# Seven block products for the last batch's outputs as well, and earlier or later places for three groups of sums

## The chip, the cores and the metric

The kernel runs on one core of a Trainium2 chip. The core has five engines that run their own instruction streams and meet at semaphores: TensorE (PE in the profile, its weight loads PEld) multiplies matrices, VectorE (DVE), ScalarE (ACT) and GpSimd (POOL) work on tiles, and SyncE (SP) issues the transfers. Each stream is in order: an instruction that waits holds everything behind it on its engine. On-chip data lie in SBUF, results of TensorE in PSUM. The metric is device time in microseconds of one execution, lower is better; all arithmetic is in float32.

## The reference

There are 8 batches of 256 tokens of width 1024, and 32 heads of width 32. Keys and values are the same tensor, 256 rows for each batch.

```python
mu, var = mean(hidden), var(hidden)
x = (hidden - mu) * rsqrt(var + 1e-05) * ln_gamma + ln_beta
Q = split_heads(x @ Wq.T)                      # 8, 32, 256, 32
K = V = split_heads(memory)
scores = einsum('bhsd,bhtd->bhst', Q, K) * 32 ** -0.5
scores = where(mask, scores, -inf)
attn = einsum('bhst,bhtd->bhsd', softmax(scores), V)
out = hidden + merge_heads(attn) @ Wout.T
```

## The kernel before

**Slots.** The work is cut into 64 slots, eight for each batch; a slot is four heads of one batch. Slot n (the loop at L887) issues the scores of slot n + 1 (L479), the value products of slot n - 2 (L622), a piece of the previous batch's output product and a piece of the query product of a later batch, all on TensorE, and the softmax of slot n + 1 on the other engines. Batch b's own slots are 8b to 8b + 7; its outputs are computed in the eight or nine slots after them.

**Softmax.** For each head VectorE adds the mask bias and takes the maximum of the (negated) scores (L515), ScalarE takes the exponential with its sum (L519), VectorE the reciprocal of the sum (L526), GpSimd multiplies (L528), and VectorE transposes 32x32 blocks (L534). ScalarE copies a part aside (L540) and SyncE moves blocks between partitions by four transfers (L600, L604; the loads of the slot, called `between`, go out in the middle). ScalarE also copies attended values from PSUM (`copy_at`, L635).

**Products by seven.** Where two matrices are cut in 2x2 blocks, their product is made from seven block products instead of eight, with sums of blocks ahead and behind. For the queries of batches 3 to 7 the blocks of x are summed on GpSimd (`sum_x`, L430): S1 = A21 + A22, S2 = S1 - A11, S4 = A12 - S2, S3 = A22 - S2. The seven products (L440) of a batch lie in seven successive slots, the first of them two slots into the batch before it. For the outputs of batches 0 to 6 the same is done with the attended values (`sum_at`, L675; products at L694 in `product_steps`), where S3 = A11 - A21, S2 = A22 - S3, S1 = S2 + A11, S4 = A12 - S2. Token halves are the rows, halves of the 1024 inner columns the columns of A; Wout is cut in B11, B12, B21, B22, from which T1 to T4 are built by GpSimd in the first slots (`sum_wo`), T1 in the place of B12. The same sums of the query weights (`sum_wq`, L391) are written over the weights; three blocks are stored in DRAM and come back through the tile `ring` (`keep_wq`, `load_ring`).

**Order of outputs.** In a batch's second slot TensorE makes A11 x B11 for the batch before (po_A, L694), ScalarE copies it to p1 (`keep_p1`, L702), and only then TensorE may go on adding A12 x B21 into the same PSUM tile. Other sums are added from PSUM by VectorE (L732, L736) or from p1 by GpSimd (L727) to the residual tiles `r`.

**Normalized x.** SyncE loads x, VectorE takes its statistics (L226) and block transpose (L311), and 16 transfers (`move_x`, L327) bring the blocks to their partitions (tile xnT). The tables `moves`, `sums`, `away` and `rings` say by hand in which slot each step is issued. For batches 4 to 7, S1 of x is issued at the end of the slot before a batch's first, for the next batch; S2 at the end of the first slot, after S3 of the attended values; S4 and the S2 of the values in the second. For batch 3 its S1 is in slot 16, and S2 and S4 in slot 17.

**The last batch.** Its outputs are plain: for two token halves and two column halves, eight products of 128x512 each (`project`, L744). B12 is loaded again into the query weights' place (`load_b12`, L753). Four products of the first output are made inside the loop; the others follow it, with the values of slots 62 and 63 between them. The residual is loaded into `again` (L1013) after the loop; VectorE adds (L736, L1037) and SyncE stores. The last output is split into 384 and 128 columns.

Of the kernel before, what the change touches and what calls it, by code (L numbers as in the profile page):

```python
# [46 lines left out]
F32 = mybir.dt.float32  # L47
U8 = mybir.dt.uint8
AF = mybir.ActivationFunctionType
ALU = mybir.AluOpType  # L50

P = 128
# [7 lines left out]
def xattn_kernel(  # L60
# [11 lines left out]
    nc = tc.nc  # L72
    B, S, D = x.shape
    T = mask.shape[2]
    HD = D // HEADS
    NC = D // P
    NQ = NC
    NH = P // HD
    NS = S // P
    NT = T // P  # L80
    NO = D // 512
# [5 lines left out]
    N = B * NQ  # L87

    const = ctx.enter_context(tc.tile_pool(name="const", bufs=1))
    xp = ctx.enter_context(tc.tile_pool(name="xp", bufs=2))  # L90
# [12 lines left out]
    ps_s = ctx.enter_context(tc.tile_pool(name="ps_s", bufs=4, space=PS))  # L103
    ps_v = ctx.enter_context(tc.tile_pool(name="ps_v", bufs=2, space=PS))
    ps_q = ctx.enter_context(tc.tile_pool(name="ps_q", bufs=1, space=PS))
    ps_o = ctx.enter_context(tc.tile_pool(name="ps_o", bufs=1, space=PS))

    NK = D // P // 2
    ring = const.tile([P, NK, NK, P], F32, tag="ring", name="ring")
# [13 lines left out]
    xs, ks, vs, rs = {}, {}, {}, {}  # L123
# [300 lines left out]
    def sum_x(b, name):  # L424

        one, two, op = {
            "S1": ("A21", "A22", ALU.add), "S2": ("S1", "A11", ALU.subtract),
            "S4": ("A12", "S2", ALU.subtract), "S3": ("A22", "S2", ALU.subtract),
        }[name]
        nc.gpsimd.tensor_tensor(x_part(b, name), x_part(b, one), x_part(b, two), op)  # L430
# [229 lines left out]
    def operand(b, name):  # L660

        if name in ("S2", "S1"):
            return s2s[b]
        s, k = {"A11": (0, 0), "A12": (0, 1), "A21": (1, 0), "A22": (1, 1),
                "S3": (1, 0), "S4": (0, 1)}[name]
        return ats[b, k][:, :, s].rearrange("p c a k -> p c (a k)")

    def sum_at(b, name, c=slice(0, NK)):
        if name == "S2" and c.start == 0:
            s2s[b] = up.tile([P, NK, P], F32, tag="s2", name=f"s2_{b}")  # L670
        one, two, op = {
            "S3": ("A11", "A21", ALU.subtract), "S2": ("A22", "S3", ALU.subtract),
            "S1": ("S2", "A11", ALU.add), "S4": ("A12", "S2", ALU.subtract),
        }[name]
        nc.gpsimd.tensor_tensor(  # L675
            operand(b, name)[:, c], operand(b, one)[:, c], operand(b, two)[:, c], op
        )
# [56 lines left out]
    def store(b, s, h, po=None):  # L734
        r = rs.pop((b, s, h))
        nc.vector.tensor_tensor(r, pos[b] if po is None else po, r, ALU.add)  # L736
        nc.sync.dma_start(out[b, ts(s, P), ts(h, 512)], r)

    def project(po, b, s, h, chunks, cols=slice(0, 512)):

        for c in chunks:
            k, i = divmod(c, NK)
            w = {(0, 0): wo[:, B11], (1, 0): wo[:, B21], (1, 1): wo[:, B22], (0, 1): b12}[k, h]
            nc.tensor.matmul(  # L744
                po, ats[b, k][:, i, s].rearrange("p a k -> p (a k)"), w[:, i, cols],
                start=(c == 0), stop=(c == NC - 1),
            )


    b12 = wq[:, :2].rearrange("p o c q -> p (o c q)").rearrange("p (c q) -> p c q", c=NK)  # L750

    def load_b12(c):
        nc.sync.dma_start(b12[:, c], woT[ts(c, P), ts(1, 512)])  # L753

# [19 lines left out]
    for b in range(1, B):  # L776
        first = NQ * (b - 1) + 2
        if b == 1:
            when = dict(moves=())
        elif b == 2:  # L780
            when = dict(
                loads=(0, 1), stats=(2, 3), norms=(3, 3), trans=(4, 5),
                moves=tuple(5 + i // 4 for i in range(16)),
            )
        else:
            when = dict(
                loads=(first - 12, first - 11) if b == SPLIT else (first - 13, first - 12),
                stats=(first - 10, first - 9) if b == SPLIT else (first - 11, first - 9),
                norms=(first - 8, first - 7), trans=(first - 7, first - 6),
                moves=tuple(first - 6 + (i + 2) // 6 for i in range(16)),  # L790
            )
        for table, key in (
            (loads, "loads"), (stats, "stats"), (norms, "norms"), (trans, "trans"),
        ):
            for i, n in enumerate(when.get(key, ())):
                assert n < first
                table[n].append((b, i))
        for n in range(N):
            part = [i for i, slot in enumerate(when["moves"]) if slot == n]
            if part:  # L800
                assert n < first - 1
                moves[n].append((b, part))
        biases[NQ * b - 2].append(b)
        if b % 2 == 0:
            masks[NQ * b - 7].append(b)
# [7 lines left out]
    ):  # L813
        sums[n] += [partial(sum_wo, which, c) for c in chunks]
    for n, which, *chunks in (
        (9, "T1", 0), (14, "T1", 1, 2), (15, "T1", 3), (15, "T3", 0, 1), (16, "T3", 2),
        (18, "T3", 3), (19, "T2", 0), (20, "T2", 1, 2, 3), (21, "T4", 0, 1), (22, "T4", 2, 3),
    ):
        sums[n] += [partial(sum_wq, which, o) for o in chunks]


    away, rings = {n: [] for n in range(N)}, {n: [] for n in range(N)}
    for n, name, half in (
        (9, "B11", 0), (10, "B11", 1), (15, "T1", 0), (16, "T1", 1), (16, "T3", 0), (19, "T3", 1),
    ):
        away[n].append(partial(keep_wq, name, half))
    for n, b in firsts.items():
# [53 lines left out]
    def project_steps(n, place):  # L881
        for one in steps.get((n, place), ()):
            product_steps(*one)


    last = None
    for n in range(N):  # L887
        b, i = divmod(n - NQ, NQ)
        new_q = new_qs[n]
# [15 lines left out]
        if n < NQ:  # L905
# [1 line left out]
                (B12, 0), (B22, 0), (B11, 0), (B12, 1), (B22, 1), (B11, 1), (B21, 0), (B21, 1)  # L907
            )[n]
            between.append(partial(load_wo, which, pair))
        if N - NQ <= n < N - NQ + NK:  # L910
            between.append(partial(load_b12, n - (N - NQ)))

        if n + 1 < N:
            scores(n + 1)
# [51 lines left out]
        for one in biases[n]:  # L966
            mask_bias(one)
        project_steps(n, 2)
        if b >= 0:
            for name in {0: ("S3",), 2: ("S4",), 3 if b == B - 2 else 5: ("S1",)}.get(i, ()):  # L970
                sum_at(b, name)
            if i == 0 and b == B - 2:
                sum_at(b, "S2", slice(0, NK - 1))
        for slot, name in ((n + 3, "S1"), (n + 2, "S2"), (n + 1, "S4"), (n - 1, "S3")):
            if slot in firsts and firsts[slot] > SPLIT:
                sum_x(firsts[slot], name)
        for slot, name in ((n + 2, "S1"), (n + 1, "S2"), (n + 1, "S4"), (n - 1, "S3")):
            if firsts.get(slot) == SPLIT:
                sum_x(SPLIT, name)
        if b == B - 2:  # L980
            if i > 2:
                add_kept(b, i, *ENDS_TO[i])
# [9 lines left out]
            fold(n)  # L992
        for one in sums[n]:
            one()
        if not new_qs[n] and N - NQ + 2 < n < N - 1:

            chunks = [c for c in range(NQ) if N - NQ + c <= n - 3]
            if last is None:
                last = ps_q.tile([P, 512], F32, tag="pq", name="po_last")
                made = 0  # L1000
            project(last, B - 1, 0, 0, chunks[made:])
            made = len(chunks)


    send(B - 2, *ENDS_TO[7])
    add_kept(B - 2, 2, *ENDS_TO[2])
    send(B - 2, *ENDS_TO[2])
    ends = [(B - 1, s, h) for h in range(NO) for s in range(NS)]
    pos = {end: ps_s.tile([P, 512], F32, tag="sc", name=f"po_{end[1]}_{end[2]}") for end in ends[1:]}
    pos[ends[0]] = last  # L1010
    again = xp.tile([P, NS, D], F32, tag="x", name="x_again")
    for s in range(NS):
        nc.sync.dma_start(again[:, s, :], x[B - 1, ts(s, P), :])  # L1013
    for b, s, h in ends:
        rs[b, s, h] = again[:, s, ts(h, 512)]
    project(pos[ends[1]], *ends[1], range(NK))
    project(last, *ends[0], range(made, NQ - 3))
    values(N - 2)
    copy_at(N - 2)
    project(pos[ends[1]], *ends[1], range(NK, NQ - 3))  # L1020
    project(pos[ends[2]], *ends[2], range(NK))
    project(last, *ends[0], (NQ - 3,))
    project(pos[ends[1]], *ends[1], (NQ - 3,))
    values(N - 1)
    copy_at(N - 1)
    project(pos[ends[2]], *ends[2], range(NK, NQ - 1))
    for i, end in enumerate(ends[:3]):
        project(pos[end], *end, range((NQ - 2, NQ - 2, NQ - 1)[i], NQ))
        store(*end, pos[end])

    b, s, h = ends[3]
    r = rs.pop(ends[3])
    for cols in (slice(0, 384), slice(384, 512)):
        po = pos[ends[3]] if cols.start == 0 else ps_v.tile([P, P], F32, tag="pv", name="po_end")
        po = po[:, : cols.stop - cols.start]
        project(po, *ends[3], range(NQ), cols)
        nc.vector.tensor_tensor(r[:, cols], po, r[:, cols], ALU.add)  # L1037
        nc.sync.dma_start(out[b, ts(s, P), ds(512 * h + cols.start, cols.stop - cols.start)], r[:, cols])


# [38 lines left out]
```

## Time and profile before

| what | value |
|---|---|
| median of 3 runs | 592.53 us (591.06 to 595.61) |
| the profiled execution | 590.59 us |
| its span, first to last instruction | 588.8 us |
| mean granted TensorE clock | 0.994 |
| TensorE busy | 572.1 us, 97% of the span |
| VectorE, ScalarE, GpSimd busy | 453.9, 412.1 and 396.7 us |
| transfers | 119.02 MB, mean 202 GB/s |

A row of a timeline gives start, length, engine, line, operation, output tile <- input tiles, shapes and the number of merged records; brackets hold the idle time of the engine before it and what ended that. One float32 product of 128x512 has two records, about 0.43 us each. In the list of waits, the numbers behind a pair are total us, times and the longest. A row by stretch gives the stretch, its length, then busy us and (records) for PE, PEld, DVE, ACT and POOL, the granted clock (1.00 is full speed), the share of the transfer engines and GB/s.

### The profile page before, as it was taken

What the parts mean: (1) busy time and instruction counts of PE and PEld (TensorE: products, weight loads), DVE (VectorE), ACT (ScalarE), POOL (GpSimd) and SP (SyncE); (2) the same over time, 40 slices, a digit from 0 to 9 for tenths busy, and PEclk for the clock granted to TensorE, in tenths of its full rate; (3) what the DMA queues carried; (4) which work ended last, traced back from release to release, by engine and by line L of the source; (5) the groups of instructions that cost most, each with busy time, mean ns of one, the idle gap of its engine ahead of it and who ended that gap; (6) DMA issues with size and microseconds to landing.
All of it is one profiled execution on the core that took longest, in us unless ns stands there. A gap on an engine that the chain in (4) does not pass through costs nothing.

```text
span 588.8 us, 20015 instructions
## 1 busy us (share of the span) xinstructions
PE 572.1 (97%) x7176; PEld 395.1 (67%) x7176; DVE 453.9 (77%) x1686; ACT 412.1 (70%) x1424; POOL 396.7 (67%) x663
## 2 busy tenths in 40 slices
PE   8999998999999999899999999799998999999997
PEld 8778884676676776577766776467774777754544
DVE  6898898787778887888888888678876778779801
ACT  4688877776578775796777877578775766769810
POOL 1787999789788985766576762857628466458720
PEclk9999999999999999999999999999998999999999
DMA  8675798755886777876878666776657764547661
GB/s 291 240 217 174 218 259 230 248 154 171 248 247 175 236 207 220 226 221 175 241 210 245 190 186 187 241 211 201 169 140 224 221 203 141 143 121 224 177 184 71
DMA packets 48051, 119.02 MB, mean 202 GB/s; under 512 B 9168, under 2 KB 9936, under 8 KB 47952
## 3 DMA queue, kind: packets, MB, share of 16 engines
q1 hardware_dynamic: 47664, 117.74, 67.8%
q8 instruction: 57, 0.93, 0.8%
q14 instruction: 42, 0.34, 0.2%
q10 hardware_dynamic: 288, 0.01, 0.0%
HBM read 66.33 MB, written 11.53 MB: 132 GB/s over the span
## 4 chain that ended last, share of the span: by engine, by line
PE 71%; DVE 7%; DMA 6%; POOL 6%; issue 4%; ACT 3%; SPq 2%; POOLq 0%; DVEq 0%; ACTq 0%
PE po_S L694 16%; PE pq L340 9%; PE pq_A L440 9%; PE sc L479 9%; PE pv L622 8%; PE po_A L694 7%; PE pq_S L440 6%; POOL e L528 4%; DMA pT<-pT 3%; PE po L744 3%; DVE pT L534 3%; ACT e L519 2%; DVE e L515 2%; DMA x<-in_x_dram 1%; PE po_last L744 1%
## 5 line engine op out<-in xcount | busy, mean ns | idle before, releaser
L528 POOL TENSOR_SCALAR e<-e,rden 128x256 f32<-128x256 f32 x512 | 236.4, 482 | 124.5 <-DVE rden L526 123.1
L519 ACT ACTIVATE e<-e,mn 128x256 f32<-128x256 f32 x512 | 254.0, 501 | 54.6 <-DVE mn L515 54.6
L534 DVE STREAM_TRANSPOSE pT<-e 128x512 f32<-128x512 f32 x256 | 180.8, 706 | 60.1 <-POOL e L528 51.1
L515 DVE CUSTOM_DVE_ANT_0 e<-sc,mb 128x256 f32<-128x256 f32 x512 | 186.0, 416 | 32.6 <-PE sc L479 32.3
L540 ACT COPY pc<-pT 128x512 f32<-128x512 f32 x128 | 79.0, 617 | 78.9 <-DVE pT L534 39.8
L519 ACT ACTIVATION_READ_ACCUMULATOR e<-e,mn 128x1 f32 x512 | 97.8, 191 | 0.0
L340 PE MATMUL pq<-xnT,wq 128*128 128x256 f32 (+1 forms) x368 | 84.2, 383 | 2.4 <-DMA xnT<-xe 2.4
L340 PEld LDWEIGHTS pq<-xnT,wq 128*128 128x128 f32 x368 | 68.6, 190 | 17.1 <-issue 3.8
L479 PEld LDWEIGHTS sc<-k,qa 32*128 32x128 f32 x1024 | 46.4, 185 | 43.6 <-issue 25.5
L622 PE MATMUL pv<-pT,v 64*32 64x128 f32 x4096 | 74.5, 274 | 0.0
L694 PE MATMUL po_S<-wo,at 128*128 128x512 f32 x152 | 74.3, 606 | 0.0
L622 PEld LDWEIGHTS pv<-pT,v 64*32 64x32 f32 x4096 | 57.2, 105 | 25.3 <-issue 11.9
L479 PE MATMUL sc<-k,qa 32*128 32x256 f32 x1024 | 74.0, 402 | 0.1
L694 PE MATMUL po_A<-wo,at 128*128 128x512 f32 x128 | 63.9, 635 | 9.6 <-ACT p L702 8.1
L694 PE MATMUL po_S<-wo,s 128*128 128x512 f32 x104 | 50.1, 605 | 0.0
L694 PEld LDWEIGHTS po_A<-wo,at 128*128 128x128 f32 x128 | 23.2, 195 | 36.0 <-issue 22.8
L515 DVE DVE_READ_ACCUMULATOR2_ANT mn<- 128x1 f32 x512 | 42.6, 83 | 0.0
L526 DVE RECIPROCAL rden<-den 128x2 f32<-128x2 f32 x256 | 37.7, 147 | 5.7 <-ACT e L519 4.5
L440 PEld LDWEIGHTS pq_A<-xnT,wq 128*128 128x128 f32 x320 | 37.3, 192 | 4.8 <-issue 4.1
L694 PEld LDWEIGHTS po_S<-wo,at 128*128 128x128 f32 x152 | 25.8, 190 | 19.8 <-issue 19.1
L440 PE MATMUL pq_A<-xnT,wq 128*128 128x128 f32 x320 | 37.3, 275 | 0.0
L635 ACT COPY at<-pv 128x128 f32<-128x128 f32 x128 | 26.2, 254 | 10.3 <-PE pv L622 10.3
(89 smaller groups left out, 595.3 us busy)
## 6 DMA issues: line engine op xcount, KB each, us to landing
v<-in_kv_dram SPq DMA_DIRECT2D x32, 512.0 KB, 5.2
pT<-pT SPq DMA_DIRECT2D x128, 128.0 KB, 3.3
pT<-pc SPq DMA_DIRECT2D x128, 128.0 KB, 4.4
ring<-kept_T SPq DMA_DIRECT2D x18, 512.0 KB
k<-in_kv_dram SPq DMA_DIRECT2D x32, 256.0 KB, 3.9
x<-in_x_dram SPq DMA_DIRECT2D x14, 512.0 KB
r<-in_x_dram SPq DMA_DIRECT2D x28, 256.0 KB, 5.1
out_dram<-r SPq DMA_DIRECT2D x28, 256.0 KB, 3.0
```

The source lines that it names most:

```text
L340: nc.tensor.matmul(pqs[n], wq[:, o, c, :], xnTs[b](c), start=(c == 0), stop=(c == NC - 1),)
L440: nc.tensor.matmul(pqs[b][:, o, :], w[:, c], x_[:, c], start=begins and o + c == 0, stop=c == NK - 1, skip_group_check=True,)
L479: nc.tensor.matmul(scs[n][j][:, s, :], qa[r, n % NQ, ts(s, P)], ks[n - n % 2][r, n % 2, :], start=True, stop=True,)
L515: nc.vector.tensor_tensor_reduce(out=e[:, s, :], in0=pss[j][:, s, :], in1=mbs[n // NQ], scale=1.0, scalar=NO_SCORE, op0=ALU.add, op1=ALU.m ...
L519: nc.scalar.activation(e[:, s, :], e[:, s, :], AF.Exp, bias=mn[:, s : s + 1], scale=-1.0, accum_out=den[:, s : s + 1],)
L526: nc.vector.reciprocal(rden, dens[j])
L528: nc.gpsimd.tensor_scalar(es[j][:, s, :], es[j][:, s, :], rden[:, s : s + 1], 1.0, ALU.mult, ALU.mult,)
L534: nc.vector.transpose(pT[:, :, :, j, :, :].rearrange("p a i s k -> p (a i) s k"), es[j].rearrange("p s (b t) -> p b s t", t=K),)
L540: nc.scalar.copy(pc[:, :, ts(j, 2)], pT[:, 1, :, ts(j, 2)])
L622: nc.tensor.matmul(pvs[n][r][j * HD : (j + 1) * HD], vs[n - n % 2][ts(r, 2 * K), i, ds(n % 2 * P + j * HD, HD)], pT[ts(r, 2 * K), :, i, j, ...
L635: nc.scalar.copy(ats[b, k][:, c, :, ts(r, 2), :], pv.rearrange("p a s k -> p s a k"))
L694: nc.tensor.matmul(po, operand(b, name)[:, c], wo[:, which, c], start=begins and c == 0, stop=c == NK - 1, skip_group_check=not begins,)
```

## The change

Batch 7's outputs are made by the seven products too. Its S3 is issued in slot 62. A11 x B11 is still made in the loop, in the four places that the first output had. After the loop, ScalarE copies it to `end_p1` in `ring`, which is free by then; S2, S1 and S4 go to three more parts of `ring`, chunk by chunk as the attended values arrive: chunks 0 and 1 at once and chunk 2 on GpSimd, chunk 3 on VectorE. Products go in the order of the chunks' arrival; S2 x T2 of the last chunk is multiplied twice, into two sums. The residual is loaded in slot 60, and B12 is not loaded again.

Other places: S1 of x for batches 4 to 7 goes one slot later, to the batch's first slot, ahead of S2; batch 3's S2 goes to slot 16, one earlier. S3 of the attended values goes from the next batch's first slot to the batch's own seventh (batches 2 to 6), for batch 1 to its eighth; batch 0 keeps its place. The 16 moves of batch 2 go 4, 6 and 6 to slots 5, 6 and 7 instead of 4 each to slots 5 to 8. T3 of the query weights is summed one chunk in each of slots 15 to 18, and its first half stored in slot 17 instead of 16.

```diff
+    end_sums = {"S1": ring[:, 0], "S2": ring[:, 1], "S4": ring[:, 2]}
+    end_p1 = ring[:, 3].rearrange("p c q -> p (c q)")
...
+    def end_sum(chunks, engine):
+        for name, one, two, op in (
+            ("S2", "A22", "S3", ALU.subtract), ("S1", "S2", "A11", ALU.add),
+            ("S4", "A12", "S2", ALU.subtract),
+        ):
+            engine.tensor_tensor(
+                end_operand(name)[:, chunks], end_operand(one)[:, chunks],
+                end_operand(two)[:, chunks], op,
+            )
+
+    def end_steps(po, name, which, chunks, begins=(), cols=slice(0, 512)):
 
         for c in chunks:
...
             nc.tensor.matmul(
-                po, ats[b, k][:, i, s].rearrange("p a k -> p (a k)"), w[:, i, cols],
-                start=(c == 0), stop=(c == NC - 1),
-            )
...
+                po, end_operand(name)[:, c], wo[:, which, c, cols],
+                start=c in begins, stop=True, skip_group_check=True,
+            )
+
+    def end_add(r, po):
+        nc.vector.tensor_tensor(r, po, r, ALU.add)
...
-                moves=tuple(5 + i // 4 for i in range(16)),
+                moves=tuple(5 + (i + 2) // 6 for i in range(16)),
...
-        (9, "T1", 0), (14, "T1", 1, 2), (15, "T1", 3), (15, "T3", 0, 1), (16, "T3", 2),
-        (18, "T3", 3), (19, "T2", 0), (20, "T2", 1, 2, 3), (21, "T4", 0, 1), (22, "T4", 2, 3),
+        (9, "T1", 0), (14, "T1", 1, 2), (15, "T1", 3), (15, "T3", 0), (16, "T3", 1),
+        (17, "T3", 2), (18, "T3", 3), (19, "T2", 0), (20, "T2", 1, 2, 3), (21, "T4", 0, 1), (22, "T4", 2, 3),
...
+    S3_SLOTS = [(b, NQ * b + {0: NQ, 1: NQ - 1}.get(b, NQ - 2)) for b in range(B)]
...
-        (9, "B11", 0), (10, "B11", 1), (15, "T1", 0), (16, "T1", 1), (16, "T3", 0), (19, "T3", 1),
+        (9, "B11", 0), (10, "B11", 1), (15, "T1", 0), (16, "T1", 1), (17, "T3", 0), (19, "T3", 1),
...
-        if N - NQ <= n < N - NQ + NK:
-            between.append(partial(load_b12, n - (N - NQ)))
+        if n == N - 4:
+            again = xp.tile([P, NS, D], F32, tag="x", name="x_again")
+            for s in range(NS):
+                between.append(partial(nc.sync.dma_start, again[:, s, :], x[B - 1, ts(s, P), :]))
...
+        for one, slot in S3_SLOTS:
+            if n == slot:
+                sum_at(one, "S3")
         if b >= 0:
-            for name in {0: ("S3",), 2: ("S4",), 3 if b == B - 2 else 5: ("S1",)}.get(i, ()):
+            for name in {2: ("S4",), 3 if b == B - 2 else 5: ("S1",)}.get(i, ()):
                 sum_at(b, name)
...
-        for slot, name in ((n + 3, "S1"), (n + 2, "S2"), (n + 1, "S4"), (n - 1, "S3")):
-            if slot in firsts and firsts[slot] > SPLIT:
+        for slot, name in ((n + 2, "S1"), (n + 2, "S2"), (n + 1, "S4"), (n - 1, "S3")):
+            if slot in firsts:
                 sum_x(firsts[slot], name)
-        for slot, name in ((n + 2, "S1"), (n + 1, "S2"), (n + 1, "S4"), (n - 1, "S3")):
-            if firsts.get(slot) == SPLIT:
-                sum_x(SPLIT, name)
...
+    nc.scalar.copy(end_p1, last)
+    end_sum(slice(0, 2), nc.gpsimd)
+    nc.gpsimd.tensor_tensor(r00, r00, end_p1, ALU.add)
+    nc.gpsimd.tensor_tensor(r01, r01, end_p1, ALU.add)
...
+    for c in range(2):
+        end_steps(to_c11, "A12", B21, (c,), (0,))
+        end_steps(to_c21, "A22", T4, (c,), (0,))
     values(N - 2)
     copy_at(N - 2)
...
+    end_sum(slice(2, 3), nc.gpsimd)
+    end_steps(last, "S3", T3, range(NK))
+    end_add(r10, last)
+    end_add(r11, last)
+    s2t2 = ps_o.tile([P, 512], F32, tag="po", name="po_end_s2")
+    end_steps(s2t2, "S2", T2, range(2), (0,))
     values(N - 1)
     copy_at(N - 1)
...
+    end_sum(slice(3, 4), nc.vector)
+    first_cols, last_cols = slice(0, 384), slice(384, 512)
+    end_steps(to_c22, "S1", T1, range(2), (0,))
+    end_steps(s2t2, "S2", T2, (2,))
+    for r in (r01, r10, r11):
+        end_add(r, s2t2)
+    end_steps(to_c22, "S1", T1, (2,))
+    end_steps(to_c11, "A12", B21, (2,))
+    end_steps(to_c21, "A22", T4, (2,))
+    end_steps(to_c22, "S2", T2, (3,))
+    end_steps(to_c22, "S1", T1, (3,))
+    end_add(r11, to_c22)
+    end_store(1, 1)
+    end_add(r01, to_c22)
+    end_steps(to_c21, "A22", T4, (3,))
+    end_steps(to_c21, "S2", T2, (3,))
+    end_add(r10, to_c21)
+    end_store(1, 0)
+    end_steps(to_c11, "A12", B21, (3,))
+    end_add(r00, to_c11)
+    end_store(0, 0)
+
+    for cols in (first_cols, last_cols):
+        po = to_c12[:, cols] if cols.start == 0 else ps_v.tile([P, P], F32, tag="pv", name="po_end")
+        end_steps(po, "S4", B22, range(NK), (0,), cols)
+        end_add(r01[:, cols], po)
+        end_store(0, 1, cols)
```

More of the change, by code (lines that the diff above doesn't have):

```diff
@@ L737, in store, with end_operand @@
         nc.sync.dma_start(out[b, ts(s, P), ts(h, 512)], r)
-    def project(po, b, s, h, chunks, cols=slice(0, 512)):
+    end_sums = {"S1": ring[:, 0], "S2": ring[:, 1], "S4": ring[:, 2]}
+    end_p1 = ring[:, 3].rearrange("p c q -> p (c q)")
+    def end_operand(name):
+        return end_sums[name] if name in end_sums else operand(B - 1, name)
+    def end_sum(chunks, engine):
[8 more added lines that the diff above has]
+    def end_steps(po, name, which, chunks, begins=(), cols=slice(0, 512)):
         for c in chunks:
-            k, i = divmod(c, NK)
-            w = {(0, 0): wo[:, B11], (1, 0): wo[:, B21], (1, 1): wo[:, B22], (0, 1): b12}[k, h]
             nc.tensor.matmul(
-                po, ats[b, k][:, i, s].rearrange("p a k -> p (a k)"), w[:, i, cols],
-                start=(c == 0), stop=(c == NC - 1),
-            )
-    b12 = wq[:, :2].rearrange("p o c q -> p (o c q)").rearrange("p (c q) -> p c q", c=NK)
-    def load_b12(c):
-        nc.sync.dma_start(b12[:, c], woT[ts(c, P), ts(1, 512)])
+                po, end_operand(name)[:, c], wo[:, which, c, cols],
+                start=c in begins, stop=True, skip_group_check=True,
+            )
+    def end_add(r, po):
+        nc.vector.tensor_tensor(r, po, r, ALU.add)
     START = 3
@@ L883, in project_steps @@
             product_steps(*one)
-    last = None
     for n in range(N):
@@ L994, in xattn_kernel @@
             one()
-        if not new_qs[n] and N - NQ + 2 < n < N - 1:
-            chunks = [c for c in range(NQ) if N - NQ + c <= n - 3]
-            if last is None:
+        if N - NQ + 2 < n < N - 1:
+            c = n - (N - NQ + 3)
+            if c == 0:
                 last = ps_q.tile([P, 512], F32, tag="pq", name="po_last")
-                made = 0
-            project(last, B - 1, 0, 0, chunks[made:])
-            made = len(chunks)
+            end_steps(last, "A11", B11, (c,), (0,))
     send(B - 2, *ENDS_TO[7])
@@ L1007, in xattn_kernel @@
     send(B - 2, *ENDS_TO[2])
[L1008 to L1017, printed above, removed]
+    r00, r01, r10, r11 = (again[:, s, ts(h, 512)] for s in range(NS) for h in range(2))
@@ new lines, in end_store @@
+    def end_store(s, h, cols=slice(0, 512)):
+        nc.sync.dma_start(
+            out[B - 1, ts(s, P), ds(512 * h + cols.start, cols.stop - cols.start)],
+            again[:, s, ds(512 * h + cols.start, cols.stop - cols.start)],
+        )
[3 more added lines that the diff above has]
+    nc.gpsimd.tensor_tensor(r01, r01, end_p1, ALU.add)
+    to_c11, to_c21, to_c22, to_c12 = (
+        ps_s.tile([P, 512], F32, tag="sc", name=f"po_end_{i}") for i in range(4)
+    )
@@ L1018, in xattn_kernel @@
+    for c in range(2):
+        end_steps(to_c11, "A12", B21, (c,), (0,))
+        end_steps(to_c21, "A22", T4, (c,), (0,))
     values(N - 2)
     copy_at(N - 2)
[L1020 to L1023, printed above, removed]
+    end_sum(slice(2, 3), nc.gpsimd)
[3 more added lines that the diff above has]
+    s2t2 = ps_o.tile([P, 512], F32, tag="po", name="po_end_s2")
@@ L1024, in xattn_kernel @@
+    end_steps(s2t2, "S2", T2, range(2), (0,))
     values(N - 1)
     copy_at(N - 1)
[L1026 to L1038, printed above, removed]
+    end_sum(slice(3, 4), nc.vector)
```

## The prediction

> **What bounds the kernel now.** I read the page's busy table first, then the list of waits, then the timelines of TensorE and GpSimd round TensorE's gaps, then the granted clock there.
>
> ```profile
> PE 572.1 (97%) x7176; PEld 395.1 (67%) x7176; DVE 453.9 (77%) x1686; ACT 412.1 (70%) x1424; POOL 396.7 (67%) x663
> ```
>
> TensorE (PE) is busy 97% of 588.8 us and no other engine passes 77%: the time is TensorE's work plus 16.7 us of gaps. The list of waits (total us, times, longest) says who ends them:
>
> ```profile
> POOL sx L430 <- DMA xnT<-xe: 18.4, 3, 6.7
> PE po_A L694 <- ACT p L702: 8.1, 4, 2.3
> PE pq L340 <- DMA xnT<-xe: 2.4, 1, 2.4
> PE po_A L694 <- DVE r L736: 1.3, 2, 1.2
> ```
>
> The last three are 11.8 us of TensorE gaps; the rest lies in the first and last microseconds. The timeline of TensorE (start, length) gives their places:
>
> ```profile
> 102.79 3.69 PE L340 MATMUL pq<-xnT,wq 128*128 128x256 f32 x16 [2.41 <-DMA xnT<-xe]
> ...
> 238.52 2.84 PE L694 MATMUL po_A<-wo,at 128*128 128x512 f32 x6 [2.33 <-ACT p L702]
> ...
> 307.84 2.84 PE L694 MATMUL po_A<-wo,at 128*128 128x512 f32 x6 [1.13 <-ACT p L702]
> 372.57 3.70 PE L694 MATMUL po_A<-wo,at 128*128 128x512 f32 x8 [1.16 <-DVE r L736]
> 379.68 4.14 PE L694 MATMUL po_A<-wo,at 128*128 128x512 f32 x6 [2.32 <-ACT p L702]
> ...
> 452.06 4.54 PE L694 MATMUL po_A<-wo,at 128*128 128x512 f32 x6 [2.33 <-ACT p L702]
> ```
>
> The first is batch 2's first query matmul waiting for its transposed x. The others (with 0.16 at 444.95) sit in the second slot of batches 3, 4, 5 and 6, 9.43 us together. What ScalarE was late with there, GpSimd shows at the third:
>
> ```profile
> 368.50 1.27 POOL L430 TENSOR_TENSOR sx<-xnT 128x512 f32<-128x512 f32 x1 [6.70 <-DMA xnT<-xe]
> 369.72 0.55 POOL L234 TENSOR_TENSOR rstd<-ve,mhalf 128x1 f32<-128x1 f32 x1
> 370.26 1.84 POOL L528 TENSOR_SCALAR e<-e,rden 128x256 f32<-128x256 f32 x4
> ```
>
> GpSimd is in order: S1 of the next batch's x (L430) stood before the moves had landed, and the normalization (L528) queued behind it started at 370.26 although its divisor was computed at 366.12 on VectorE. VectorE's transposes wait for that, its next reductions stand behind them, ScalarE's exponentials and its copy of p behind those. Delays of the first normalization at the four places (its start less 0.1 after its divisor's): 2.9, 1.5, 4.0 and 3.3 us; TensorE's gaps there: 2.3, 1.1, 3.5 and 2.5.
>
> Batch 2's second slot is the control, since batch 3's S1 already sits one slot later:
>
> ```profile
> 161.18 1.29 POOL L675 TENSOR_TENSOR at<-at 128x512 f32<-128x512 f32 x1
> 162.41 1.29 POOL L430 TENSOR_TENSOR sx<-xnT 128x512 f32<-128x512 f32 x1
> 163.64 1.30 POOL L391 TENSOR_TENSOR wq<-wq 128x512 f32<-128x512 f32 x1
> ```
>
> Three sums, 3.9 us, after the normalizations, and TensorE's next po_A, at 167.87, has no gap. Nor has the boundary at 520, where no x follows.
>
> **Part 1: S1 of x one slot later, S3 two slots earlier.** Batches 4 to 7: S1 leaves the slot before. In the first slot GpSimd then does S1 and S2 (2 x 1.27) where it did S3 and S2: the same length at the same place, less than the control carries. Would S1 wait there? In the worst case the moves land at 368.5; the four normalizations, begun at 366.3, end about 370.6. Margin 2 us. What is late next: at the gap of 238.52 everything moves 2.9 us earlier, the copy of p ends at 235.6 and TensorE has finished its values at 236.1; at the other three I get margins of 0.4 to 0.6 the same way. So all 9.43 goes, thinly covered: each 0.5 us by which S1 + S2 delay the next divisor comes back at four places.
>
> S3 (1.27) moves into the seventh slot of batches 2 to 7, the eighth of batch 1. Its last operand is copied a slot before (270.39 in batch 3, where the sum will stand near 283.9). GpSimd idles 4.2 us there in batch 3 (before 288.18), 1.33 us in batch 2 (before 217.50): there the cover is 0.06 us, and half of S3 lost there would be 0.6. Taken at nothing. Batch 3's S2 joins its S1 in slot 16, and with the shuffled sums of the query weights slots 15, 16 and 17 keep three long sums each, as before: nothing. The stored half of T3 is one SP issue (about 0.5 us) a slot later, behind the transposes' transfers and three slots ahead of its reload: nothing.
>
> **Part 2: batch 2's moves in three slots.** 16 issues of about 0.6 us, now 4, 6 and 6. The last began at 98.26 and landed at 102.7. They will follow the second group (90.80) and end about 95.3, landed near 98, while TensorE wants them at 100.4: 2.41 us gone. What they pass on SP: two more issues push slot 6's pT transfers 0.9 us (SP idled 0.37 ahead of 77.54) and slot 8's 1.2 us, which are wanted by value products a slot later. Nothing; 1.2 if that cover fails.
>
> **Part 3: the clock.** The same three matmuls took 2.84 us after two of the gaps, 4.14 and 4.54 after the others. The granted clock by stretch (the column after POOL):
>
> ```profile
> 238.00:243.00 5.00, 4.48 (x67) 2.41 (x71) 4.03 (x11) 2.91 (x10) 4.61 (x7) 1.00 0.83 244
> ...
> 379.00:384.00 5.00, 4.32 (x10) 1.59 (x14) 4.06 (x9) 3.07 (x11) 4.61 (x8) 0.71 0.74 250
> ...
> 452.00:457.00 5.00, 4.94 (x14) 1.96 (x18) 2.20 (x4) 2.45 (x9) 4.29 (x6) 0.66 0.85 269
> ```
>
> The slow stretches cost 1.30 + 1.70, and the scores behind the first 0.34 (1.42 for 1.08): 3.3 us. The Trainium skill (TensorE: Matmul & The Clock Gate, "What's actually happening") has the clock fall to half after an idle window of about 3.4 us, and "Why this matters for your kernels" warns of gaps over about 3 us only. By that rule these gaps of 2.3 us cost no clock and the whole sum below is 13.9 us; by the rows it is 17.2. I take the rows. The page also says the window runs freely, so other executions may lose more or less: 0 to 1.7 for each of five gaps over 2 us, 0 to 8.5 in all.
>
> **Part 4: the end.** After the loop TensorE now does 28 products of 128x512 (0.86 each: six records take 2.57) and two sets of values (1.09 each), without a gap, from 558.8 to 585.74. Then an addition of 0.29, a store, and the end at 588.8. After the change I count 25: 8 for A12B21 and A22T4, 4 for S3, 3 for S2T2 and its last chunk twice, 4 for S1, 4 for S4 (24 of seven products less A11's four, done in the loop, and one repeat). Less 3 x 0.86 = 2.6. The end stays addition and store of 128 columns.
>
> Waits on the way: the second chunk of A12 and A22 stands at 560.6, and its copy ends at 561.08 on ScalarE (0.44 from 560.64): 0.5 lost. GpSimd: S3 from 558.8 (no trace shows the half-width sum; 128x128 took 0.46 and 128x384 1.00, so 0.73), three kept additions to 563.9, three half sums to 566.1, two additions of p1 to 568.6, three quarter sums to 570.0; S2's third chunk is wanted at 572.1. The last chunk: values end at 570.3, copy 570.8, three sums on VectorE (nearest row 0.29, from PSUM; between 0.2 and 0.46) 571.7; wanted at 575.6. VectorE's nine additions of 0.69 lie between matmuls, each behind a different bank. x again: loaded at about 549.6 instead of 566.7, two issues (0.9) on SP in a wait of 1.0 for pT to land; the pc transfer behind takes 4.4 by the page's median, so 555.7, wanted at 557.7. The four loads of B12 (0.43 each on SP) go: nothing. So the end is worth 2.1 (from 2.6 if no wait, to -1.5 if the sums come 3.5 later than I have them).
>
> **The sum.** 9.4 + 2.4 + 3.3 + 2.1 = 17.2. The profiled execution took 590.59 (span 588.8 and 1.8 round it): 573.4. The median of the runs is 1.94 above it, so 592.53 - 17.2 = 575.3.
>
> **Rivals.** A measurement of this kernel can tell about 1%, 5.9 us, from no change.
>
> *A new wait at the boundaries.* S1 + S2 hold the next normalization, the 0.5 us margins are used up, and half of the 9.4 + 3.3 stays. For it: margins this thin. Against: the control with 3.9 us of sums and no gap. Gain 2.4 + 2.1 + 6.4: 581.6.
>
> *The end gives nothing or loses.* Chunk by chunk it hangs on copies and sums that the plain products did not need. Gain 15.1 less up to 1.5: 577.4 to 579. Against: margins of 2 and 4 us above.
>
> *Slower.* S3 in the seventh slot waits on GpSimd for its operand, as S1 did for its moves, and normalization queues behind it in seven batches. At the price of today's gaps, 12.7 / 4 = 3.2 each, that is 22.3, against 17.2 removed: 597.6. It decides if the fourth copy comes after GpSimd's normalizations of that slot; against it stand the 13 us of part 1.
>
> *It does not do what it says:* S1 still waits, now in the first slot, since the moves hang on something I misread, and only the end and batch 2 gain: 588.
>
> **Chances.** Forecast 0.64; new wait 0.17; end 0.12; nothing at the boundaries 0.04; slower 0.03. Faster by over 1%: 0.93, within 1%: 0.04, slower: 0.03. Range 572 to 582: below, another 3.3 us of clock recovered; above, the new wait's time.
>
> **What would show it.** The sum S1 starts without idle time before it in a batch's first slot; no po_A gap over 0.3 us at L694 in a second slot; the first query matmul of batch 2 without a wait for xnT; a granted clock of 1.00 throughout; the end from 558.8 (in today's count) about 2 us shorter with one gap of 0.5 us. Wrong if GpSimd's S1 row keeps a wait for xnT, if ScalarE's copy of p still ends TensorE's gaps, or if the additions of VectorE end the last stretch.

## The result, and the profile after

The changed kernel takes 575.4 us in the median (572.83 to 579.34, 4 runs), against 593.16 before (591.06 to 595.61, 4 runs): ratio 0.9705, 95% interval [0.9635, 0.9775]. The forecast was 575.3. In two later comparisons the changed kernel took 575.21 and 575.96, at 0.9834 [0.9758, 0.991] and 0.9782 [0.9731, 0.9833]; there the kernel before stood at 588.3 and 590.2. (A ratio leaves out executions more than 1.5% above the fastest of their kernel, so it can differ from the quotient of the medians.) What the change saves lies, by the three ratios, between 9.8 and 17.5 us, according to the executions of the kernel before that it is compared with; the changed kernel's own median stayed within 1 us from one comparison to the next.

The profiled execution of the changed kernel took 579.34 us (span 577.6), the slowest of its four; its profile shows a part of the reason. The page's busy table first:

```profile
PE 567.7 (98%) x7162; PEld 392.2 (68%) x7162; DVE 458.6 (79%) x1695; ACT 412.1 (71%) x1425; POOL 404.7 (70%) x672
```

TensorE has 14 records less: batch 7's outputs take 33 matmuls of two records each where they took 40. Behind the loop that is the work of 25 matmuls of 128x512 instead of 28 (the last four are split in two, so 29 are issued). VectorE and GpSimd got the sums. TensorE's gaps by its timeline (start, length, then the work behind the gap):

```profile
98.06 1.13 PE L694 MATMUL po_A<-wo,at 128*128 128x512 f32 x2 [1.71 <-DMA wo<-in_woT_dram]
...
243.75 1.87 PE L694 MATMUL po_A<-wo,at 128*128 128x512 f32 x2 [2.19 <-issue]
...
552.05 1.98 PE L761 MATMUL po_end<-wo,at 128*128 128x512 f32 x4 [0.36 <-ACT at L635]
```

All that stood in the forecast's list of gaps is gone: the four places with `ACT p` or `DVE r`, and the wait for xnT. Of the three shown, two were not foreseen: a wait for the second load of B21 (the half of B21 that was loaded in slot 7) at 98.06, and 2.19 us at 243.75 that nothing ends in the profile. The third is the half microsecond foreseen behind the loop. Three more new gaps, of 0.2 to 0.3 us, are left out. GpSimd's list of waits has no entry for S1 or S2 of x any more. Its timeline at the boundary of batch 3 (the rows at 368.50 before were batch 5's, the same place in the program):

```profile
229.45 1.85 POOL L528 TENSOR_SCALAR e<-e,rden 128x256 f32<-128x256 f32 x4 [0.57 <-DVE rden L526]
231.26 1.27 POOL L430 TENSOR_TENSOR sx<-xnT 128x512 f32<-128x512 f32 x1
232.60 1.28 POOL L430 TENSOR_TENSOR sx<-sx,xnT 128x512 f32<-128x512 f32 x1
234.54 1.85 POOL L528 TENSOR_SCALAR e<-e,rden 128x256 f32<-128x256 f32 x4 [0.66 <-DVE rden L526]
```

S1 and S2 stand behind the slot's normalizations, without idle time before S1, and the next normalization waits for its divisor, not for them: 0.66 us are to spare. The granted clock by stretch (stretch, length, busy us of PE, PEld, DVE, ACT, POOL, clock, share of the transfer engines, GB/s):

```profile
100.00:238.00 138.00, 137.40 (x1734) 93.74 (x1727) 111.55 (x414) 100.92 (x348) 115.14 (x177) 1.00 0.74 218
...
244.00:249.00 5.00, 5.00 (x27) 3.97 (x27) 2.96 (x13) 2.73 (x12) 1.79 (x4) 0.69 0.86 276
...
254.00:577.00 323.00, 320.31 (x4182) 213.68 (x4181) 253.64 (x934) 227.14 (x799) 203.38 (x355) 1.00 0.66 190
```

The clock fell behind the 2.19 us gap, so one sign named ahead, a clock of 1.00 throughout, did not hold. The two groups of matmuls there took 1.87 and 4.54 us; in the next profile of the same kernel, at full clock, 1.02 and 3.73. The other three executions report 1.000 (571.0, 572.5 and 574.7 us of span).

### The profile page after: what moved, and what is told of

Read it like the earlier page. It is cut to its first block, busy times and chain, and to the rows that moved or that the text cites. A ratio compares the mean times of both kernels' runs of the same rounds, so it can differ in the third digit from the quotient of the medians.

```text
span 577.6 us, 20001 instructions
## 1 busy us (share of the span) xinstructions
PE 567.7 (98%) x7162; PEld 392.2 (68%) x7162; DVE 458.6 (79%) x1695; ACT 412.1 (71%) x1425; POOL 404.7 (70%) x672
## 4 chain that ended last, share of the span: by engine, by line
PE 79%; POOL 8%; DVE 6%; issue 2%; DMA 2%; ACT 1%; SPq 0%; DVEq 0%; POOLq 0%; ACTq 0%
PE po_S L694 17%; PE pq_A L440 16%; PE sc L479 10%; PE po_A L694 10%; PE pv L622 9%; PE pq_S L440 6%; POOL e L528 6%; PE pq L340 6%; DVE e L515 3%; PE po_end L761 2%; DVE pT L534 1%; PE po_last L761 1%; POOL wo L183 1%; DMA pT<-pT 1%; ACT e L519 1%
## 5 line engine op out<-in xcount | busy, mean ns | idle before, releaser
L694 PE MATMUL po_A<-wo,at 128*128 128x512 f32 x128 | 61.9, 616 | 4.2 <-issue 2.2
```

The costliest lines, as they stand in the source:

```text
L694: nc.tensor.matmul(po, operand(b, name)[:, c], wo[:, which, c], start=begins and c == 0, stop=c == NK - 1, skip_group_check=not begins,)
```

## The experiments

Each is the kernel before or the changed kernel with one edit. Ratios are against the kernel before in the same comparison.

### The end alone

The changed kernel with the sums' places, batch 2's moves and T3's sums of before; what is left of the change is the last batch. One line of the edit; the others put back lines of before that the diff above shows:

```diff
...
-    S3_SLOTS = [(b, NQ * b + {0: NQ, 1: NQ - 1}.get(b, NQ - 2)) for b in range(B)]
+    S3_SLOTS = [(b, NQ * b + {B - 1: NQ - 2}.get(b, NQ)) for b in range(B)]
...
```

> Only the end of the changed kernel (seven products for batch 7, its S3 in slot 62, the residual loaded in slot 60); S1 and S3 sums of the other batches, batch 2's moves and the T3 sums as before. My theory: the end is worth 2.1 us and the gaps in the second slots of batches 3 to 6 stay, with the clock they cost: ratio 0.9965. Rival (the end is worth what the 17.8 us lack elsewhere): over 5 us, ratio under 0.992.

Measured: 591.07 us against 591.84, ratio 0.9961 [0.9922, 1.0001]. By the ratio 2.3 us, not over 5; the interval just reaches no change, so the size rests on the profiles: TensorE's work behind the loop takes 24.95 us in this kernel (562.61 to 587.56) and in the changed one (549.71 to 574.66), where it was 26.95 before: 2.0. The boundaries keep their gaps (TensorE's timeline of this kernel):

```profile
242.06 4.43 PE L694 MATMUL po_A<-wo,at 128*128 128x512 f32 x6 [2.33 <-ACT p L702]
...
314.56 2.84 PE L694 MATMUL po_A<-wo,at 128*128 128x512 f32 x6 [2.33 <-ACT p L702]
```

The same gap of 2.33 us is followed by slow matmuls at one place (4.43 us for 2.84) and not at the other.

### S1 of x later, alone

The kernel before, with S3 left where it was.

```diff
-        for slot, name in ((n + 3, "S1"), (n + 2, "S2"), (n + 1, "S4"), (n - 1, "S3")):
+        for slot, name in ((n + 2, "S1"), (n + 2, "S2"), (n + 1, "S4"), (n - 1, "S3")):
```

> The kernel before with one edit: S1 of x for batches 4 to 7 one slot later; S3 of the attended values stays in the same slot, so GpSimd does three sums (3.8 us) there. My theory: S1 no longer waits, but the three sums hold the next divisor's normalization by about 0.9 us against margins of 0.5: gaps of about 0.4 us at four places instead of 9.4 in all, no clock lost; 11 us faster, ratio 0.981. Rival (S3's move is what frees the boundary): under 6 us, ratio over 0.990. Rival (the three sums matter not, as in the control): 12.7 us, ratio 0.9785, no gap.

Measured: 581.66 us, ratio 0.98 [0.9742, 0.9857], 11.8 us by the ratio. That lies between my figure and that of the second rival, and the time can't tell them apart; the profile does. No second slot of batches 3 to 6 has a gap, so the three sums cost TensorE nothing there. On GpSimd they do hold the next normalization, which follows with no idle time (its divisor was there by 239.0, the normalization starts at 239.61):

```profile
235.78 1.27 POOL L675 TENSOR_TENSOR at<-at 128x512 f32<-128x512 f32 x1
237.00 1.28 POOL L430 TENSOR_TENSOR sx<-xnT 128x512 f32<-128x512 f32 x1
238.36 1.28 POOL L430 TENSOR_TENSOR sx<-sx,xnT 128x512 f32<-128x512 f32 x1
239.61 1.85 POOL L528 TENSOR_SCALAR e<-e,rden 128x256 f32<-128x256 f32 x4
```

and yet TensorE does not notice (the same slot on TensorE):

```profile
239.97 1.16 PE L622 MATMUL pv<-pT,v 64*32 64x128 f32 x64
241.06 2.84 PE L694 MATMUL po_A<-wo,at 128*128 128x512 f32 x6
```

The copy of p stands on ScalarE behind exponentials of that same softmax, and VectorE's reductions for them (from 236.76) come ahead of the transposes that need the normalization (from 241.27); the copy ends at 240.92. So a late normalization delays the copy of the slot after it, not of its own. My margin of 0.5 us was set against the wrong sum.

### S3 earlier, alone

The kernel before, with S3 of batches 2 to 6 in the batch's own seventh slot and S1 where it was.

```diff
-            for name in {0: ("S3",), 2: ("S4",), 3 if b == B - 2 else 5: ("S1",)}.get(i, ()):
+            for name in {0: ("S3",) if b < 2 else (), 2: ("S4",), 3 if b == B - 2 else 5: ("S1",)}.get(i, ()):
...
+        if i == 6 and 1 <= b < B - 2:
+            sum_at(b + 1, "S3")
```

> The kernel before with one edit: S3 of the attended values of batches 2 to 6 in the batch's own seventh slot; S1 of x stays. My theory: S1 still waits for the moves, the gaps stay, at most 1 us gained: ratio 0.998 to 1.000, granted clock of the executions below 1.00 in some. Rival (S3's move frees the boundary): 6 us or more, ratio under 0.990.

Measured: 592.34 us, ratio 0.9983 [0.9929, 1.0038]; as expected. S1 still waits (GpSimd, then TensorE two slots later):

```profile
230.32 1.28 POOL L430 TENSOR_TENSOR sx<-xnT 128x512 f32<-128x512 f32 x1 [4.74 <-DMA xnT<-xe]
```

```profile
241.52 2.84 PE L694 MATMUL po_A<-wo,at 128*128 128x512 f32 x6 [1.75 <-ACT p L702]
```

The two experiments together show that S1's place makes the boundary's gain, and that S3's move alone makes none that the time can show. The new places of the query weights' T3 and of batch 3's S2 were not tried alone; TensorE has no gap from 150 to 176 us, where they stand, before or after.

### Batch 2's moves, alone and taken back

Alone, in the kernel before:

```diff
-                moves=tuple(5 + i // 4 for i in range(16)),
+                moves=tuple(5 + (i + 2) // 6 for i in range(16)),
```

> The kernel before with one edit: batch 2's 16 moves in slots 5, 6 and 7 (4, 6, 6). My theory as recorded: 2.4 us, ratio 0.996, the first query product of batch 2 without a gap. What the profile after suggests: the second load of B21 lands later and TensorE waits about 1.7 us for it one slot earlier, so 0.4 to 0.7 us, ratio 0.999.

Measured: 590.08 us, ratio 0.9974 [0.9935, 1.0012]: no answer by the time. The profile has no wait for xnT; one slot ahead it has 0.82 us for a copy on ScalarE and 0.49 for B21. The same edit taken back in the changed kernel:

> The changed kernel with batch 2's moves back at 4 each in slots 5 to 8. My theory: the gap of about 2.4 us before batch 2's first query product comes back and the wait for the second load of B21 goes; against the changed kernel of the same call 0 to 1 us slower. Rival (the load's wait has nothing to do with the moves): the wait for B21 stays and 2.4 us come on top.

Measured: 578.49 us (576.39 to 580.74), ratio 0.9888 [0.9823, 0.9952]; the changed kernel in the same comparison 575.21 (574.02 to 577.54). So 3.3 us slower by the medians, more than either theory, and the ranges overlap a little. The wait for B21 is gone and that for xnT is back, longer than in the profile that the forecast read:

```profile
103.36 3.69 PE L340 MATMUL pq<-xnT,wq 128*128 128x256 f32 x16 [3.12 <-DMA xnT<-xe]
```

Over all profiles with the old moves this gap is 2.41, 3.36, 3.99, 4.15 and 3.12 us, 3.4 in the mean. With the new ones TensorE's gaps from 85 to 107 us add up to 2.2, 1.3 and 2.2 in the changed kernel's three profiles and to 1.7 with the moves alone, 1.9 in the mean. So the moves save about 1.5 us of gaps, and most of what they give back is the wait for B21. They lengthen that wait and are not its only cause: S1 later alone, with the old moves, has 0.53 us of it.

The gaps are not all. In three of the five profiles with the old moves the matmuls behind this gap were slow as well: 5.38 us (the end alone), 6.34 (S1 later) and 5.38 (S3 earlier) for 3.69. The longest, with a granted clock of 0.50 from 105 to 110 us:

```profile
105.39 6.34 PE L340 MATMUL pq<-xnT,wq 128*128 128x256 f32 x16 [3.99 <-DMA xnT<-xe]
```

That is 1.2 us in the mean of the five. With it the moves are worth about 2.7 us by the profiles, which lies near the 3.3 of the medians.

### Why B21 lands late

Two cures. First, its two loads one slot earlier:

```diff
...
-                (B12, 0), (B22, 0), (B11, 0), (B12, 1), (B22, 1), (B11, 1), (B21, 0), (B21, 1)
-            )[n]
+            (0, B12, 0), (1, B22, 0), (2, B11, 0), (3, B12, 1), (4, B22, 1), (5, B11, 1),
+            (5, B21, 0), (6, B21, 1),
...
```

> The changed kernel with the two loads of B21 one slot earlier (slots 5 and 6 instead of 6 and 7). My theory: the load has landed when TensorE wants it, the gap of 1.7 us before A12 x B21 goes, nothing else moves: 1.5 us faster than the changed kernel of the same call. Rival (the transfer engines are full from 82 to 94 us whatever the order, and something else lands late): no difference.

Measured: 578.0 us (576.3 to 578.89) against the changed kernel's 575.21: a miss for my theory, and by the medians worse than the rival too, though the ranges overlap a little. The wait for B21 is gone, and a longer one took its place. First TensorE, then VectorE, which caused it:

```profile
93.41 5.40 PE L694 MATMUL po_A<-wo,at 128*128 128x512 f32 x8 [3.75 <-ACT qa L349]
```

```profile
89.78 0.69 DVE L226 BATCH_NORM_STATS2 st<-x 128x6 f32<-128x512 f32 x1 [3.92 <-DMA x<-in_x_dram]
```

The statistics of batch 3's x, in the middle of a softmax on VectorE, now wait longer for their load. It was issued at 84.38 us, in the changed kernel at 81.23: with two weight loads ahead of them in slot 5, SyncE's six moves took 6.85 us instead of 3.76, and the load stands behind them. ScalarE's copy of the query waits for that softmax, and TensorE for the copy. The matmuls behind the gap took 5.40 us, for 3.70 at full clock; the granted clock was 0.66 there. So the second cure leaves B21 and takes batch 3's x away from it: x's loads and statistics one slot later.

```diff
-                loads=(first - 12, first - 11) if b == SPLIT else (first - 13, first - 12),
-                stats=(first - 10, first - 9) if b == SPLIT else (first - 11, first - 9),
+                loads=(first - 11, first - 10) if b == SPLIT else (first - 13, first - 12),
+                stats=(first - 9, first - 8) if b == SPLIT else (first - 11, first - 9),
```

> The changed kernel with batch 3's loads of x and their statistics one slot later (loads in slots 7 and 8 instead of 6 and 7, statistics in 9 and 10 instead of 8 and 9), so that 1 MB less is ahead of the second load of B21 while the transfer engines are full. My theory: B21 has landed in time, the gap of 1.0 to 1.7 us in slot 9 goes; 1 to 2 us faster than the changed kernel of the same call. Rival: as when B21 was moved, another transfer lands late in its place (now the statistics' x in slot 9): no gain or a loss.

Measured: 572.95 us (572.52 to 573.35), ratio 0.9733 [0.9682, 0.9783]; the changed kernel in the same comparison 575.96 (573.64 to 577.7). That is 3.0 us less by the medians, with ranges that don't touch, and faster than both kernels. In the profile (span 571.2) no gap is left between 9 and 238 us, where the changed kernel's third profile has 2.4 us of them:

```profile
94.55 2.84 PE L694 MATMUL po_A<-wo,at 128*128 128x512 f32 x6
...
100.45 3.62 PE L340 MATMUL pq<-xnT,wq 128*128 128x256 f32 x16
```

One of x's two loads is still issued just ahead of B21's second half (85.77 and 86.26), the other now at 96.91: 0.5 MB less is ahead of it, not the 1 MB of the expectation. In the profile after, the transfer engines are taken throughout from 86 to 94 us (by stretch, the last three columns are clock, share and GB/s; a share at or over 1 is read as full):

```profile
86.00:90.00 4.00, 3.76 (x28) 2.58 (x27) 3.81 (x10) 2.88 (x10) 3.17 (x8) 1.00 1.05 247
90.00:94.00 4.00, 4.00 (x71) 2.02 (x70) 3.11 (x19) 3.74 (x14) 4.00 (x4) 1.00 1.04 327
```

B21's second half landed 12 us after its issue there (85.9 to 98.0), 7.7 us in the kernel with x later, whose shares are 0.96 and 0.92. Of the two cures only the one that takes bytes out of that stretch helped. Why B21 is late is not settled by this: in the kernel before the shares are 1.04 and 0.98, B21 is issued at the same time (85.75), and TensorE doesn't wait for it; and the edit moved the statistics together with the loads.

### The gap that nothing ends

The changed kernel once more, and a third time:

> The changed kernel once more, as the comparison for the two others and for the gap of 2.2 us that nothing in the profile ends. My theory: that gap belongs to one execution (a late fetch of TensorE's instructions) and is not at that place in this profile; a ratio of 0.970 against the kernel before. Rival: it belongs to the kernel and stands at the same place.

> The changed kernel a third time, as the comparison for the two others. My theory: 573 to 577 us, the gap near 242 us of 0.8 to 2.2 us before the same po_A product.

The ratios stand with the result. My theory for the first of these fell: the gap stands before the same product, at 241.76, in this profile 0.83 us long (1.10 in the third), and likewise in every kernel that has S1 later (0.56 to 2.19 us) save that of the next experiment, in none that has not:

```profile
241.76 1.02 PE L694 MATMUL po_A<-wo,at 128*128 128x512 f32 x2 [0.83 <-issue]
```

So it belongs to the kernel. The profile's transfers of the queue marked "instruction" (16 KB each, 57 in a run) come about every 9 us; here one comes 14.4 to 16.1 us after the one before. In all seven profiles that have the gap it ends 1.3 to 1.5 us after that transfer does (in the profile after: 242.4, and TensorE goes on at 243.75), and always at the same count, about the 5825th of all TensorE's instructions in the trace, its waits among them (the 5726th of its loads and products). A late transfer is not enough for a gap: in the profile after, others at 47.4, 127.1 and 381.4 us come 15.3 to 15.5 us after the one before, and TensorE doesn't stop there. If these transfers bring TensorE's instructions, fewer instructions at the start must move the place:

```diff
-    for _ in range(32):
+    for _ in range(24):
         nc.tensor.transpose(busy, ident, ident)
```

> The changed kernel with 24 instead of 32 warming transposes at the very start, that is 16 fewer instructions on TensorE ahead of everything. If the gap of 0.8 to 2.2 us near 242 us, which no engine ends, is a late fetch of TensorE's instructions, it stands at the same count from the start (5825 loads and products in four profiles), that is 16 instructions later in the work: behind the po_A product, among the weight loads and products of pq_S. Rival (something in the work there): the gap stays before the same po_A product. The start may be up to 2 us longer[...].

Measured, in a single execution: 572.34 us, span 570.6. The gap is gone from the po_A product (238.26, with the transfer ending at 238.0), which speaks against something in the work there; but it does not stand 16 instructions later either. The 5825th comes at 239.78 in this profile, 1.8 us after the transfer, later than the 1.3 to 1.5 at which the others went on, so that no gap would be due. In the kernel before, TensorE stood for `ACT p` while the transfer came. All this fits a late fetch of TensorE's instructions and a gap that hangs on the position in the instruction stream, but one execution without the gap proves neither; what makes the gap stays open. This profile has no wait for B21 either (it landed 8.4 us after its issue), though nothing was changed there: how long TensorE waits for B21 is not fixed by the program's order alone. So for the kernel with x later the four executions count, and not its one profile without the wait.

## Why the prediction was right

**The boundaries.** The chain was read rightly: with S1 in its new place all four places lost their gaps, and the edit alone gave 11.8 us by its ratio against the 12.7 of the forecast (gaps and clock). The control, batch 2's boundary with three sums and no gap, was the better guide; the margins of 0.4 to 0.6 us ahead of the copy of p, and the fear for S1 + S2, rested on the step "each 0.5 us by which S1 + S2 delay the next divisor comes back". S1 later alone refutes it.

**S3.** Taken at nothing, and the time shows nothing else: 0.9983 [0.9929, 1.0038] alone, an interval of about 3 us to either side. Its cover of 0.06 us in batch 2 made no gap.

**Batch 2's moves.** The wait for xnT went as foreseen. The step that failed is "Nothing; 1.2 if that cover fails": it looked at the pT transfers that the moves pass on SyncE, and not at the loads. The second load of B21 is what came late, by 1.0 to 1.7 us in three profiles; moves alone give 0.49. The moves also went out later than forecast, the last at 98.0 in the profile after and not before 95.3; TensorE, held up by B21, wanted them only at 102.24. The term was 2.4; of gaps it is about 1.5, and the clock that the old gap cost in other profiles (1.2 in the mean of five) was not in it.

**The clock.** Taking the rows against the window of about 3.4 us (the Trainium skill, "TensorE: Matmul & The Clock Gate", section "What's actually happening") was right in kind. In the profiles of the kernel before, of the end alone, of S3 alone and of the moves alone, ten gaps of 2.33 us (2.32 in one) were followed by slow matmuls at five. The four gaps of 3.36 to 4.15 us in all profiles were all followed by them, one of 3.12 us was not. So the gaps near and above the page's figure fit it, and those of 2.33 us are not safe, as it would have them be. As the comparison for the first four experiments the kernel before ran 25 times, at granted clocks from 0.986 (600.48 us) to 1.000 (587.80 us) and over a range of 14.8 us; the changed kernel ran twelve times in all, at 0.997 to 1.000 and over 6.5 us. That part, which the sum held as 0 to 8.5 us, differs from run to run, and with it the change's gain. The clock is not the whole spread: at a reported 0.997 those executions of the kernel before took 585.68 to 592.24 us.

**The end.** 2.1 was forecast, 2.0 is measured, with the one wait that was named (0.36 for 0.5). The half sum that no trace had shown took 0.73 us as estimated, the last three sums on VectorE 0.29, as the nearest row (PSUM) gave.

**The sum.** 17.2 was forecast for the difference, from 593.16 to 575.4 it is 17.8, against the later medians of both kernels 13.1 and 14.2. Errors of both signs went into the match: about 0.9 too much for the moves' gap, nothing for the clock behind it, and 0.6 to 2.2 us for the gap at 243.75 that no step had. The forecast was also counted from 592.53 us, while the kernel before stood at 588.3 to 593.2 in four comparisons. The paths were right; that forecast and median differ by 0.1 us is luck.

## What to carry to other kernels

On an engine in order, look at what stands behind a wait for a transfer: here one sum of 1.3 us, placed a slot too early, held a normalization that three engines depend on, and one line's move was worth 12 us. A second place in the same program where the sum already stood later gave the answer before any run. And where the transfer engines were full, a load issued one slot earlier only moved the wait to another load; taking a load out of the full stretch made the kernel 3.0 us faster.

## What the runs showed of the hardware

Gaps on TensorE of 2.33 us were followed by a fall of the granted clock (to 0.66 to 0.71 over 5 us) at five of ten places, worth 1.3 to 1.7 us each at the matmuls behind; the four of 3.36 to 4.15 us always were, at 1.7 to 2.7 us each. And in seven profiles a gap of 0.56 to 2.19 us that no engine ended stood at the same count of TensorE's instructions, 1.3 to 1.5 us behind the end of a late 16 KB transfer on the instruction queue; in the one execution with 16 instructions fewer ahead of it, it was gone.
